# Cross-attention and scan in fp32: row tiles transposed by VectorE and SBUF-to-SBUF DMA instead of TensorE

## The chip, the core and the metric

The kernel runs on one core of one Trainium2 chip. The metric is the device time of one execution, in microseconds. Before the change it is 2022.62 us, the median of three runs (2022.18 to 2022.88).

## What is computed

All tensors are fp32. 4096 rows of 512 attend with 8 heads to 3202 context rows, then pass a recurrence with 64 states. The reference, cut to what matters:

```python
x = layernorm(rows, g1, beta1); base_n = layernorm(context, g1, beta1)
x = rows + mha(x, base_n, W_qkv, b_qkv, W_o, b_o)      # 8 heads of 64
xn = layernorm(x, g2, beta2)
U = (xn @ W_in.T + b_in) @ Bmat                         # 64 inputs a row
s = silu(s @ A.T) + u_t                                 # step after step, per batch
out = x + states @ Cmat + mod                           # mod: one row, from ctxb
```

## The kernel before

**Stages.** A first stage (to about 165 us of the span) normalises the context, makes keys and values, writes them to two DRAM tensors, kd and vd, and makes the first queries. The loop (to about 1880 us) does the attention. A tail runs the scan and writes the output.

**The loop.** The rows come in 8 blocks Q of 512 rows. A block has 4 head pairs hp of 2 halves of 256 rows: 8 units. A unit walks over 13 chunks of keys, its steps. A step is scores (L639, TensorE, sixteen 64x64 matmuls of 256 columns), weights (L709, exp on ScalarE), add (L717, the sum of the weights, on VectorE, in three of the steps on GpSimd) and, four steps later, product (L749, TensorE). At the end of a unit, fold (L724, GpSimd) adds two halves of the sum and sums (L767, TensorE, tile pd) reduces it over the keys. The adds of a unit are one chain: each reads the one before.

**Rows in and out.** For block Q+1, `queries` loads its rows in two halves of two tiles of 128 rows (x, L876), normalises them (statistics L843 on VectorE, factors L847 to L849 on GpSimd, scaling L855 on ScalarE to tile xh), has TensorE transpose them (`turn`: four 128x128 transposes a tile, L282, tile tp_x) and ScalarE copy them out of PSUM (L305); then four `heads` (L312) multiply them with the query weights. For block Q-1, `project` loads the rows again (xr, L924), adds a bias on GpSimd (L927, piece "row"), multiplies with W_o (`outs`, L933, tile pa), makes x1 (L943), stores x1 plus mod to DRAM (mod L947 on GpSimd, store L950), normalises, turns (tile tp_y) and multiplies with the scan's input weights (`inputs`, L984, tile pu). A turn of two tiles is one piece on TensorE.

**What sets the order.** The order is not written by hand. `Plan` holds pieces, each with an engine, a cost in ns, pieces that it comes after, a due time in steps (STEP = 2150 ns) and buffers that it takes and gives. `order` plays them through: a free engine takes, of the pieces that are ready, the one with the earliest due time. A due time holds nothing back: a free engine takes a ready piece early. The order of the calls that comes out is the order of the instructions on every engine; an engine then runs its own in that order and waits in front of the first that is not ready. Two details matter here. A TensorE piece of the full array (outs, turn, inputs, heads) counts as due 30,000 ns, 14 steps, later while no other of its kind could go (ALONE). And a result of SP counts as there 3000 ns after its piece (LATE). The loads of the keys and values (k, v; L1021, L1029) are no pieces: they are issued on SP where the scores of a step are placed, ten and six steps ahead. Every load, store and move here is on SP's queue.

Of the kernel before, what the change touches and what calls it, by code (L numbers as in the profile page):

```python
# [10 lines left out]
F32 = mybir.dt.float32  # L11
# [7 lines left out]

T, S2, H, NH, HD, NS = 4096, 3202, 512, 8, 64, 64  # L20
P = 128
NC = H // P
NCH = 26
CK = 128
# [3 lines left out]
QB = 512  # L28
# [141 lines left out]
def xattn_ssm_kernel(  # L170
# [114 lines left out]
        return tp[:, :, :n]  # L285

    xp_ = actx.enter_context(tc.tile_pool(name="xp", bufs=2))
    xnp = actx.enter_context(tc.tile_pool(name="xnp", bufs=2))
    qp = actx.enter_context(tc.tile_pool(name="qp", bufs=6))
    ps_m = actx.enter_context(tc.tile_pool(name="ps_m", bufs=1, space=PSUM))  # L290
    m_pools = [ps_m]
# [12 lines left out]
        yield  # L304
        nc.scalar.copy(xn[:, :, t * P : (t + 1) * P], tp)  # L305

    def heads(Q, hp, xns):

        pq = m_tile([P, 512], f"pq_{Q}_{hp}")
        for half in range(2):  # L310
            for i in range(NC):
                nc.tensor.matmul(  # L312
                    pq[:, half * QU : (half + 1) * QU],
                    wq[:, i, hp * P : (hp + 1) * P],
                    xns[half][:, i, :],
                    start=(i == 0),
                    stop=(i == NC - 1),
                )
# [7 lines left out]
    first_xns = []  # L326

    def first_queries(x0):

        xns = []  # L330
        for half in range(2):
            xn = xnp.tile([P, NC, QU], F32, tag="xn", name=f"xn_0_{half}")
            xns.append(xn)
            for t in range(NT // 2):
                name = f"x{half * QU + t * P}"
                last = normalize(x0[:, half * (NT // 2) + t, :], P, name, later=True)
                yield
                yield
                xh = last()
                yield  # L340
                yield
                for _ in turned(xn, xh, t, name):
                    yield
                yield
                yield
        first_xns.extend(xns)
        pieces = heads(0, 0, xns)
        next(pieces)
        for _ in pieces:
            yield  # L350
        yield
# [483 lines left out]
    def norm_pieces(plan, ks, gets, d, after, names, gives):  # L835
# [21 lines left out]
        for t, (k, v) in enumerate(zip(ks, vs)):  # L857
            plan.add((*k, "stats"), "DVE", 870, partial(stats_, v, gets[t], names[t]), [after[t]],
                     d + t, ["fs"])
            plan.add((*k, "factors"), "POOL", 1050, partial(factors_, v), [(*k, "stats")], d + 2000)  # L860
            plan.add((*k, "scaled"), "ACT", 800, partial(scaled_, v, gets[t], t),
                     [(*k, "factors")] + ([(*ks[0], "scaled")] if t else []), d + 3 * STEP + t,
                     [] if t else ["xh", "xh"], [("fs", (*k, "stats")), gives[t]])
        return vs

    def queries(plan, Q, d):

        xns, copied = [], []
        for half in range(2):
            ks = [("query", Q, half * 2 + t) for t in range(2)]  # L870
            at = [Q * QB + half * QU + t * P for t in range(2)]
            k2, vs, w = ("queries", Q, half), [{}, {}], {}

            def load(v, r):
                v["x"] = xp_.tile([P, H], F32, tag="x", name=f"x_{r}", bufs=4)
                nc.sync.dma_start(v["x"], x[r : r + P, :])  # L876
# [4 lines left out]
            nv = norm_pieces(plan, ks, [lambda v=v: v["x"] for v in vs], d, [(*k, "load") for k in ks],  # L881
                             [f"x{r}" for r in at], [("x", (*k, "load")) for k in ks])

            def turn(half=half, nv=nv, at=at, w=w):
                xn = xnp.tile([P, NC, QU], F32, tag="xn", name=f"xn_{Q}_{half}")
                xns.append(xn)
                w["turns"] = [turned(xn, nv[t]["xh"], t, f"x{at[t]}") for t in range(2)]
                for one in w["turns"]:
                    next(one)
# [8 lines left out]
        head_pieces(plan, Q, range(NC), xns, copied, d, QSTEP // 2,  # L898
                    [("xn", ("queries", Q, half, "turn")) for half in range(2)])

    def head_pieces(plan, Q, hps, xns, copied, d, apart, xn_):
        for hp in hps:
            v = {}

            def head(v=v, hp=hp):
                v["heads"] = heads(Q, hp, xns)
                next(v["heads"])

            plan.add(("heads", Q, hp), "PE", 3700, head, copied, d, ["m", "q"], xn_)
            plan.add(("q", Q, hp), "ACT", 590, lambda v=v: next(v["heads"], None),  # L910
                     [("heads", Q, hp)], d + STEP, [], [("m", ("heads", Q, hp))])
            d += apart

    def project(plan, Q, halves, d, index):

        for half in halves:
# [43 lines left out]
            for t in range(2):  # L960
                plan.add((*ks[t], "x1"), "DVE", 680, partial(x1_, vs[t], at[t]), [(*k2, "outs")],
                         d + STEP + t, [], [("m", (*k2, "outs"))])
            nv = norm_pieces(plan, ks, [lambda v=v: v["x1"] for v in vs], d + STEP, [(*k, "x1") for k in ks],
                             [f"y{r}" for r in at], [("x1", (*k2, "outs"))] * 2)
            for t in range(2):
                plan.add((*ks[t], "mod"), "POOL", 1280, partial(mod, vs[t]), [(*ks[t], "x1")], d + 2 * STEP,
                         [], [("x1", (*k2, "outs"))])
# [21 lines left out]
            def kept(t, w=w, at=at):  # L989
# [7 lines left out]
                    scale=2.0,  # L997
                )

            plan.add((*k2, "turn"), "PE", 1050, turn, [(*k, "scaled") for k in ks], d + 5 * STEP - now,  # L1000
                     ["m", "m", "xn2"], [("xh", (*ks[0], "scaled"))])
            for t in range(2):
                plan.add((*ks[t], "copy"), "ACT", 560, partial(copy, t),
                         [(*k2, "turn")] + ([(*ks[0], "copy")] if t else []), d + 6 * STEP + t, [],
                         [("m", (*k2, "turn"))])
            plan.add((*k2, "inputs"), "PE", 700, inputs, [(*k, "copy") for k in ks], d + 7 * STEP - now,
                     ["m"], [("xn2", (*k2, "turn"))])
            for t in range(2):
                plan.add((*ks[t], "kept"), "ACT", 280, partial(kept, t), [(*k2, "inputs")],
                         d + 8 * STEP + t, [], [("m", (*k2, "inputs"))])  # L1010
            d += 2 * RSTEP

    kts, vts = {}, {}
# [58 lines left out]
    def open_scan():  # L1072
# [2 lines left out]
        for k in (0, NS):  # L1075
            nc.sync.dma_start(t[k : k + NS], cmat)
        sv["c2"] = t
        one = xnp.tile([P, 8, NCK], F32, tag="xn", name="scan_1")
# [4 lines left out]
        two = xnp.tile([P, 1024], F32, tag="xn", name="scan_2")  # L1083
# [376 lines left out]
    def drain(plan):  # L1460
# [14 lines left out]
        plan.add("c2", "SP", 200, open_scan, [("heads", NQB - 1, NC - 1)], a0 - 6 * STEP, ["xn", "xn", "q"])  # L1475
# [208 lines left out]
    with tc.manual_schedule():  # L1684
        for g in range(AHEAD_K):
            load_k(*steps[g])
        for g in range(AHEAD):
# [1 line left out]
        plan = Plan(  # L1689
            dict(  # L1690
                s=2, m=2, mt=1, o=1, p=NP, acc=3, extra=4, q=6, x=4, x1=2, xn2=1, fs=2,
                xn=2, xh=2, max=2, rd=2, o_=12,
            ),
            dict(q=[("heads", 0, 0)], xn=[("first", half) for half in range(2)]),
        )
        head_pieces(plan, 0, range(1, NC), first_xns, [], 4 * STEP, 4 * STEP,
                    [("xn", ("first", half)) for half in range(2)])
# [109 lines left out]
```

## Time and profile before

| | |
|---|---|
| median of 3 runs | 2022.62 us |
| the profiled execution | 2022.73 us, span 2020.9 us |
| busy, share of the span | PE 98%, DVE 58%, ACT 57%, POOL 39% |
| granted TensorE clock | 0.995 of full, mean |
| DMA queue of SP and its like (q1) | 182,184 packets, 178.62 MB, 29.4% of 16 engines' span |
| loop, 165 to 1790 us | PE busy 1616.19 of 1625.00 us |
| turns in the loop | 28 (14 of tp_x, 14 of tp_y), one more at 1879.5 us |
| one block in the steady state | 218.96 us |

PE is TensorE, DVE VectorE, ACT ScalarE, POOL GpSimd, SP the engine that issues DMAs. A line of the timeline has the start in us from the span's start, the time that the line covers, the engine, the line of the kernel and the operation, and in brackets the idle time before it and what ended it. Neighbours of one kind are drawn together (x16), and such a line can hold waits inside.

### The profile page before, as it was taken

The numbers are of one execution on the slowest core, as the hardware profiler recorded it, in microseconds if no ns is written. First come the engines' busy times: TensorE is split into PE (matmuls) and PEld (weight loads), VectorE is DVE, ScalarE is ACT, GpSimd is POOL, SyncE is SP. The second block draws the span as 40 slices with busy tenths as digits, with TensorE's granted clock in tenths as the row PEclk, the third lists the DMA queues.
The fourth block names the chain that finished last, engine by engine and source line by source line (L and its number), as shares of the span: only waits on it lengthen the run. The fifth ranks groups of instructions, "written<-read, shape, count | busy, mean of one in ns | idle before, by whom it ended". The sixth has DMA issues, their size and how long they took to land.

```text
span 2020.9 us, 66912 instructions
## 1 busy us (share of the span) xinstructions
PE 1983.2 (98%) x29534; PEld 1324.9 (66%) x29534; DVE 1170.6 (58%) x1481; ACT 1160.3 (57%) x1530; POOL 789.3 (39%) x631
## 2 busy tenths in 40 slices
PE   8999999999999999999999999999999999999996
PEld 4445676776677667766677667766776667766764
DVE  4321366566665666566656666566656665666575
ACT  2233566566665566556656666556655665665653
POOL 2111244235533453245523553345324552345424
PEclk9999999999999999999999999999999999999998
DMA  5632322122222322122222222232212322444475
GB/s 169 192 99 68 99 79 83 54 80 90 88 67 78 97 79 67 55 62 93 81 59 80 90 88 67 78 96 79 67 55 62 93 81 59 144 136 129 130 208 192
DMA packets 187030, 190.66 MB, mean 94 GB/s; under 512 B 20904, under 2 KB 160168, under 8 KB 186732
## 3 DMA queue, kind: packets, MB, share of 16 engines
q1 hardware_dynamic: 182184, 178.62, 29.4%
q10 hardware_dynamic: 4548, 7.67, 1.2%
q8 instruction: 235, 3.85, 0.8%
q14 instruction: 63, 0.52, 0.1%
HBM read 156.32 MB, written 29.88 MB: 92 GB/s over the span
## 4 chain that ended last, share of the span: by engine, by line
PE 78%; DVE 10%; POOL 7%; issue 3%; ACT 1%; DMA 1%; DVEq 0%; POOLq 0%; ACTq 0%
PE po L749 27%; PE s L639 27%; DVE acc L717 6%; PE pq L312 5%; PE pk L588 4%; PE pv L555 4%; POOL acc L717 4%; PE pa L933 4%; PE pd L767 1%; DVE rd L802 1%; ACT p L709 1%; PE tp_x L282 1%; DVE acc L703 1%; POOL acc L724 1%; PE sm L657 1%
## 5 line engine op out<-in xcount | busy, mean ns | idle before, releaser
L709 ACT ACTIVATE p<-s,shifts 128x1024 f32<-128x1024 f32 (+1 forms) x832 | 894.1, 1081 | 522.8 <-PE s L639 510.4
L717 DVE TENSOR_TENSOR acc<-p,acc 128x1024 f32<-128x1024 f32 (+1 forms) x515 | 620.0, 1204 | 406.9 <-POOL acc L717 310.6
L639 PE MATMUL s<-q,k 64*64 64x256 f32 x12800 | 841.4, 378 | 2.7 <-ACT p L709 1.1
L749 PE MATMUL po<-p,v 64*64 64x256 f32 x12800 | 823.2, 376 | 0.0
L717 POOL TENSOR_TENSOR acc<-p,acc 128x1024 f32<-128x1024 f32 x189 | 446.9, 2365 | 809.1 <-DVE acc L717 484.1
L639 PEld LDWEIGHTS s<-q,k 64*64 64x64 f32 x12800 | 483.9, 133 | 217.2 <-issue 21.4
L749 PEld LDWEIGHTS po<-p,v 64*64 64x64 f32 x12800 | 489.5, 133 | 189.0 <-issue 2.2
L724 POOL TENSOR_TENSOR acc<-acc 128x512 f32<-128x512 f32 x64 | 104.5, 1633 | 135.8 <-DVE acc L717 118.0
L717 DVE TENSOR_TENSOR acc<-p,p 128x1024 f32<-128x1024 f32 x64 | 84.6, 1322 | 60.1 <-ACT p L709 54.1
L312 PE MATMUL pq<-xn,wq 128*128 128x256 f32 x512 | 119.0, 385 | 0.0
L802 DVE RECIPROCAL rd<-rd 128x256 f32<-128x256 f32 (+1 forms) x65 | 112.4, 1729 | 2.2
L312 PEld LDWEIGHTS pq<-xn,wq 128*128 128x128 f32 x512 | 94.6, 190 | 23.2 <-issue 11.6
L933 PE MATMUL pa<-wo,o 128*128 128x512 f32 x240 | 107.0, 599 | 0.0
L782 DVE TENSOR_TENSOR o<-po,o 128x256 f32<-128x256 f32 x64 | 27.2, 424 | 128.4 <-ACT o L778 128.2
L555 PE MATMUL pv<-wv,ct 128*128 128x512 f32 (+1 forms) x208 | 96.4, 616 | 1.0 <-ACT ct L523 0.7
L588 PE MATMUL pk<-ct,wk 128*128 128x512 f32 (+1 forms) x224 | 88.8, 549 | 0.0
L321 ACT ACTIVATE q<-pq,bias 128x512 f32<-128x512 f32 x32 | 22.0, 687 | 108.6 <-PE pq L312 108.6
L933 PEld LDWEIGHTS pa<-wo,o 128*128 128x128 f32 x240 | 44.4, 190 | 56.0 <-issue 55.8
L703 DVE TENSOR_TENSOR acc<-x,acc 2x256 f32<-2x256 f32 x128 | 78.1, 610 | 3.0
L523 DVE COPY ct<-tp_c 128x512 f32<-128x512 f32 (+1 forms) x13 | 8.5, 651 | 105.9 <-PE tp_c L282 105.9
L555 PEld LDWEIGHTS pv<-wv,ct 128*128 128x128 f32 (+1 forms) x208 | 38.3, 193 | 44.5 <-issue 41.7
L588 PEld LDWEIGHTS pk<-ct,wk 128*128 128x128 f32 x224 | 39.2, 190 | 42.6 <-issue 42.6
(213 smaller groups left out, 1224.1 us busy)
## 6 DMA issues: line engine op xcount, KB each, us to landing
k<-kd SPq DMA_DIRECT2D x432, 128.0 KB, 2.2
v<-vd SPq DMA_DIRECT2D x432, 128.0 KB, 2.2
xr<-in_x_dram SPq DMA_DIRECT2D x32, 256.0 KB, 4.5
x1d<-xr SPq DMA_DIRECT2D x32, 256.0 KB, 2.2
x<-in_x_dram SPq DMA_DIRECT2D x28, 256.0 KB, 3.2
cx<-in_ctx_dram SPq DMA_DIRECT2D x25, 256.0 KB, 3.0
vd<-vs SPq DMA_DIRECT2D x25, 256.0 KB, 2.4
kd<-ks SPq DMA_DIRECT2D x48, 128.0 KB, 1.8
```

The costliest lines, as they stand in the source:

```text
L312: nc.tensor.matmul(pq[:, half * QU : (half + 1) * QU], wq[:, i, hp * P : (hp + 1) * P], xns[half][:, i, :], start=(i == 0), stop=(i == NC ...
L555: nc.tensor.matmul(pv[h * HD : h * HD + n, :H], ct[:, k, o : o + n], wv[:, k, :], start=(i == 0), stop=(i == NC // parts - 1), skip_group_ ...
L588: nc.tensor.matmul(pk[:, :n_g], wk[:, i, hp * P : (hp + 1) * P], ct[:, i, :n_g], start=(i == 0), stop=(i == NC - 1),)
L639: nc.tensor.matmul(s[k0 : k0 + HD, a, b, :], kts[(*w["at"][:2], c)][r, b * CK + k0 : b * CK + k0 + HD], q[r], start=True, stop=True, skip_ ...
L703: nc.vector.tensor_tensor(to[r], t[r], to[r], ALU.add)
L709: nc.scalar.activation(t[:, :, :nb, :], w["ps"][c][:, :, :nb, :], AF.Exp, bias=w["shift"])
L717: engine.tensor_tensor(w["acc"][:, :, :nb, :], t[:, :, :nb, :], before[:, :, :nb, :], ALU.add)
L724: nc.gpsimd.tensor_tensor(acc[:, :, 0, :], acc[:, :, 0, :], acc[:, :, 1, :], ALU.add)
L749: nc.tensor.matmul(w["po"][a * HD : (a + 1) * HD, k, :QU], vts[Q, hp, c][r, b, a * HD : (a + 1) * HD], t[r, a, b, :], start=(c == 0 and b ...
L782: nc.vector.tensor_tensor(o, w["po"][:, 1, :QU], o, ALU.add)
L802: nc.vector.reciprocal(w["rd"][:, part], w["rd"][:, part])
L933: nc.tensor.matmul(v["pa"], o_t[Q, c, half][:, t * P : (t + 1) * P], wo[:, c, :], start=(c == 0), stop=(c == NC - 1),)
```

## The change

The rows of the loop (all blocks but the last one's `project`) no longer pass TensorE to be transposed. A new piece `flip` on VectorE transposes each 32x32 block of xh where it stands, into the tile that held x (or x1). Sixteen DMAs a tile then put the blocks in their places, in four pieces `move0` to `move3` on SP of four DMAs each, planned at 400 ns a piece. A DMA reads 32 partitions and writes 32 partitions, in runs of 32 numbers (128 bytes): 128 runs, 16 KB. The copies by ScalarE go too. The queries of a block are one tile of 512 columns instead of two of 256, so `heads` has half as many matmuls of twice the width. `inputs` is due 14 steps after `outs` instead of 7. The x tiles are given back after the moves instead of after the scaling, and the flip of x1 comes after mod as well.

```diff
-        for half in range(2):
-            for i in range(NC):
-                nc.tensor.matmul(
-                    pq[:, half * QU : (half + 1) * QU],
-                    wq[:, i, hp * P : (hp + 1) * P],
-                    xns[half][:, i, :],
...
+        for i in range(NC):
+            nc.tensor.matmul(
+                pq,
+                wq[:, i, hp * P : (hp + 1) * P],
+                xn[:, i, :],
...
-            plan.add((*k2, "turn"), "PE", 1050, turn, [(*k, "scaled") for k in ks], d + 4 * STEP,
-                     ["m", "m", "xn"], [("xh", (*ks[0], "scaled"))])
             for t in range(2):
-                plan.add((*ks[t], "copy"), "ACT", 560, lambda t=t, w=w: next(w["turns"][t], None),
-                         [(*k2, "turn")], d + 5 * STEP + t, [], [("m", (*k2, "turn"))])
-                copied.append((*ks[t], "copy"))
+                plan.add((*ks[t], "flip"), "DVE", 700, lambda v=vs[t], n=nv[t]: flip(v["x"], n["xh"]),
+                         [(*ks[t], "scaled")], d + 4 * STEP + t, [], [("xh", (*ks[0], "scaled"))])
+                for a in range(P // TB):
+                    first = (half, t, a) == (0, 0, 0)
+                    plan.add((*ks[t], f"move{a}"), "SP", 400, partial(move_, t, a),
+                             [(*ks[t], "flip")] + ([] if first else [("query", Q, 0, "move0")]),
+                             d + (5 + 4 * t + a) * STEP, ["xn"] if first else [], [("x", (*ks[t], "load"))])
+                    copied.append((*ks[t], f"move{a}"))
...
+    def flip(to, of):
+
+        nc.vector.transpose(to, of)
+
+    def move(xn, of, a):
+
+        for b in range(P // TB):
+            nc.sync.dma_start(
+                xn[b * TB : (b + 1) * TB, :, a * TB : (a + 1) * TB],
+                of[a * TB : (a + 1) * TB].rearrange("p (c b k) -> p b c k", b=P // TB, k=TB)[:, b],
+            )
...
-            plan.add((*k2, "inputs"), "PE", 700, inputs, [(*k, "copy") for k in ks], d + 7 * STEP - now,
-                     ["m"], [("xn2", (*k2, "turn"))])
+            if last:
...
+            else:
+                copied, xn2, after = [], (*ks[0], "move0"), 14
...
+                for t in range(2):
+                    plan.add((*ks[t], "flip"), "DVE", 700, lambda v=vs[t], n=nv[t]: flip(v["x1"], n["xh"]),
+                             [(*ks[t], "scaled"), (*ks[t], "mod")], d + 5 * STEP + t, [],
+                             [("xh", (*ks[0], "scaled"))])
+                    for a in range(P // TB):
+                        first = (t, a) == (0, 0)
+                        plan.add((*ks[t], f"move{a}"), "SP", 400, partial(move_, t, a),
+                                 [(*ks[t], "flip")] + ([] if first else [xn2]), d + (6 + 4 * t + a) * STEP,
+                                 ["xn2"] if first else [], [("x1", (*k2, "outs"))])
+                        copied.append((*ks[t], f"move{a}"))
+            plan.add((*k2, "inputs"), "PE", 700, inputs, copied, d + after * STEP - now, ["m"], [("xn2", xn2)])
```

More of the change, by code (lines that the diff above doesn't have):

```diff
@@ L21 @@
 P = 128
+TB = 32
 NC = H // P
@@ L324, in heads @@
         qt[Q, hp] = t
-    first_xns = []
+    first_xn = []
     def first_queries(x0):
[L330 to L336, printed above, removed]
-                yield
[L338 to L347, printed above, removed]
+        xn = xnp.tile([P, NC, QB], F32, tag="xn", name="xn_0")
+        first_xn.append(xn)
+        for t in range(NT):
+            name = f"x{t * P}"
+            last = normalize(x0[:, t, :], P, name, later=True)
+            yield
+            yield
+            xh = last()
+            yield
+            yield
+            for _ in turned(xn, xh, t, name):
+                yield
+            yield
+            yield
+        pieces = heads(0, 0, xn)
         next(pieces)
@@ L881, in queries @@
             nv = norm_pieces(plan, ks, [lambda v=v: v["x"] for v in vs], d, [(*k, "load") for k in ks],
[L882 to L889, printed above, removed]
@@ L901, in head_pieces, with move_ @@
-    def head_pieces(plan, Q, hps, xns, copied, d, apart, xn_):
+                             [f"x{r}" for r in at], [])
+            def move_(t, a, half=half, vs=vs):
+                if (half, t, a) == (0, 0, 0):
+                    w["xn"] = xnp.tile([P, NC, QB], F32, tag="xn", name=f"xn_{Q}")
+                c0 = (half * 2 + t) * P
+                move(w["xn"][:, :, c0 : c0 + P], vs[t]["x"], a)
+            for t in range(2):
+                plan.add((*ks[t], "flip"), "DVE", 700, lambda v=vs[t], n=nv[t]: flip(v["x"], n["xh"]),
[6 more added lines that the diff above has]
+                    copied.append((*ks[t], f"move{a}"))
@@ L1077, in open_scan @@
         sv["c2"] = t
-        one = xnp.tile([P, 8, NCK], F32, tag="xn", name="scan_1")
+        both = xnp.tile([P, 2, 1024], F32, tag="xn", name="scan")
+        one = both[:, 0, :].rearrange("p (i k) -> p i k", k=NCK)
         sv["th"] = [one[:, i, :] for i in range(2)]
@@ L1082, in open_scan @@
         sv["ok"] = one[:, 7, :]
-        two = xnp.tile([P, 1024], F32, tag="xn", name="scan_2")
+        two = both[:, 1, :]
         at_ = 0
```

58 lines of the change are left out of this document (32 added, 26 removed).

## The prediction

> **What bounds it now.** First the busy times on the page, then the list of what TensorE waited for:
>
> ```profile
> PE 1983.2 (98%) x29534; PEld 1324.9 (66%) x29534; DVE 1170.6 (58%) x1481; ACT 1160.3 (57%) x1530; POOL 789.3 (39%) x631
> ```
>
> ```profile
> PE pd L767 <- POOL acc L724: 4.9, 6, 0.8
> ```
>
> TensorE is the bound: 1616.19 of 1625.00 us in the loop. So work taken from it counts in full. But the second line (4.9 us in total, 6 times, 0.8 at the longest) is a warning: six times, once a block, `sums` already waits for the fold on GpSimd. There the chain of adds has no slack, and whatever delays it is paid by TensorE. I then read the timeline around the first block's turn, engine by engine. TensorE:
>
> ```profile
> 477.79 1.04 PE L639 MATMUL s<-q,k 64*64 64x256 f32 x16
> 478.77 1.09 PE L282 MATMUL tp_y<-ident,xh_y 128*128 128x128 f32 x8
> 479.79 1.57 PE L639 MATMUL s<-q,k 64*64 64x256 f32 x24
> 481.19 1.04 PE L749 MATMUL po<-p,v 64*64 64x256 f32 x16
> 482.05 1.04 PE L639 MATMUL s<-q,k 64*64 64x256 f32 x16
> ...
> 489.19 0.76 PE L767 MATMUL pd<-acc,ones 64*64 64x256 f32 x8 [0.81 <-POOL acc L724]
> ```
>
> Differences of the starts are what things cost: sixteen quarter matmuls 0.86 us (481.19 to 482.05).
>
> **What TensorE gains.** A turn takes 1.02 us (478.77 to 479.79). The scores ahead of it take 0.98 instead of 0.86, the 24 behind it 1.40 instead of 1.29: entering and leaving the full array is 0.23. Each of the 28 turns of the loop stands alone like this, so 28 x 1.25 = 35.0 us. A head: sixteen matmuls of 256 columns take 3.65 us (577.71 to 581.36), 0.228 each; sixteen of 512 columns (tile pa, 464.52 to 471.58) take 7.06, 0.441 each. Eight of those are 3.53, so 32 heads give 32 x 0.12 = 3.8 us. Together **38.8 us**. The profiled execution took 2022.73 us (span 2020.9 and 1.8 around it), 0.1 above the median; with nothing else it would come to 1984.
>
> **What is added off TensorE.** VectorE gets 56 flips. No such operation is in the trace. The nearest rows are VectorE's fp32 operations on 128x512: 0.48 (scaling a weight) to 0.75 us; the dearest kind, the reciprocal, takes 1.73 for 256 columns, so 3.5 is the other end. I take 0.7, as in the nearest rows: 39 us in all on an engine idle for 42% of the span; ScalarE loses 56 copies of 0.59. The idle time that hides a flip of x1 is 5.43 us from 476.26 to 481.69. At 3.5 us that cover would be gone, and the chain below would start 3 us later.
>
> **What SP gets** is the point: 56 x 16 = 896 DMAs. SP's timeline after `outs` (which ends at 471.6):
>
> ```profile
> 472.65 2.90 SPq L950 DMA_DIRECT2D x1d<-xr  x2
> 475.64 0.38 SPq L1021 DMA_DIRECT2D k<-kd  x1
> 476.12 0.40 SPq L1029 DMA_DIRECT2D v<-vd  x1
> 476.61 0.38 SPq L1021 DMA_DIRECT2D k<-kd  x1
> 477.08 0.38 SPq L1029 DMA_DIRECT2D v<-vd  x1
> 477.57 0.84 SPq L876 DMA_DIRECT2D x<-in_x_dram  x2
> ...
> 481.30 1.10 SPq L924 DMA_DIRECT2D xr<-in_x_dram  x2
> ```
>
> Back to back, one DMA follows another by 0.48 us, whether it carries 2 KB or 256 KB. No move of 32 partitions is in the trace; nearest are two DMAs into 64 partitions (tile a_t, 0.48 and 0.58 on ScalarE's queue) and one of 2 partitions (vx, 0.73). I take 0.48: 16 moves are 7.7 us, where the planner counts 1.6. As data they are light: the trace's packets last 28 ns at 512 B and 9 ns at 16 B, so eight runs of 128 B on each of 16 engines are 0.07 to 0.22 us, under the pitch. That two DMAs into parts of one tile need not wait for one another, a_t shows: issued 0.7 us apart, landing after 5.2.
>
> One rule of the Trainium skill speaks against this weight: DMA: Bandwidth & Descriptors, Issuing engines are not separate DMA queues, calls the sequencer's time to start a DMA usually small beside the DMA itself. For one k load the trace agrees (0.48 to issue, 2.2 to land); for 16 in a row the issue is 7.7. By that rule the moves would hold nothing up, and the time would be the 1984 of the first rival.
>
> **Where the moves stand in SP's order.** Due times don't spread them: a free engine takes a ready piece early. The scaling of the first tile ends at 474.79, VectorE is free at 476.26, so its flip ends near 477.0. The x loads of the next queries are released by the scores just before tp_y (477.79 to 478.77), the xr loads two to three steps later. The second tile's scaling ends at 478.20, its flip near 478.9. So the planner lays out: stores, first 16 moves, x loads, second 16 moves, xr loads, with the k and v of the steps between. Now the real times: stores until 475.55, a pair of k and v to 476.5, flip 477.0, 16 moves 7.7, two pairs 1.9, so the x loads go at 486.6 instead of 477.57, **9 us late**. Then x loads 1.0, 16 moves 7.7, two pairs 1.9: the xr loads go at 497.2 instead of 481.30, **16 us late**.
>
> **Who waits for them.** The loads' landings, and then VectorE and GpSimd, each in order:
>
> ```profile
> xr<-in_x_dram SPq DMA_DIRECT2D x32, 256.0 KB, 4.5
> ...
> x<-in_x_dram SPq DMA_DIRECT2D x28, 256.0 KB, 3.2
> ```
>
> ```profile
> 482.83 0.69 DVE L843 BATCH_NORM_STATS2 st_x<-x 128x6 f32<-128x512 f32 x1
> ...
> 484.45 0.66 DVE L717 TENSOR_TENSOR acc<-p,acc 128x512 f32<-128x512 f32 x1
> ```
>
> ```profile
> 487.87 1.26 POOL L724 TENSOR_TENSOR acc<-acc 128x512 f32<-128x512 f32 x1
> 489.09 2.51 POOL L927 TENSOR_TENSOR xr<-xr,rowb 128x512 f32<-128x512 f32 x2
> 491.55 2.38 POOL L717 TENSOR_TENSOR acc<-p,acc 128x1024 f32<-128x1024 f32 x1
> ```
>
> The statistics of x stand on VectorE in front of the last half add of a unit (484.45); that add releases the fold (487.87), the fold `sums` (489.19). The x loads landed at 481.6 (478.41 + 3.2), 1.2 us before they were needed. Nine late less 1.2: `sums` is **7.8 us** late, all of it TensorE's. Behind the fold, GpSimd adds the bias to xr (489.09), and only then comes the next unit's first add of its own (491.55), from which that unit's chain runs without a gap to its fold (ends 511.77; `sums` at 512.99, slack 1.2). The xr loads land at 497.7 + 4.5 = 502.2, so the row adds start 13.1 late; TensorE is 7.8 late already and the slack is 1.2: **4.1 more**. That is 11.9 a block, for the six blocks with both loads: 71. The last block has no queries: xr alone, one us earlier, 12.1 - 1.2 = 10.9. Together 82 us.
>
> **The rest at nothing.** The k and v of the loop are issued 13 steps, some 25 us, ahead of their use (the buffer's last reader is three steps before the issue, the use ten after); with SP late by 16 that still covers; past 25 us every further one would be lost. `inputs` stood 13.1 us after `outs` with 7 steps; with 14 it stands near 496, or 493 if another full-array piece is ready, and the second 16 moves land near 499.4 (497.2 + 2.2): 3 to 6 us short, but TensorE is 7.8 late by then and does not notice. In the blocks' second halves the x loads stand right behind the stores, ahead of the moves, and `inputs` is the only one near its limit (moves land near 551, place near 550): 0 to 5 us seven times, taken as 0. `heads` has 11 steps to spare.
>
> **Sum:** 2022.7 - 38.8 + 82 = **2066 us**.
>
> **Rivals.**
> 1. *Faster: SP's burst is hidden* (0.20), 1984 to 2010. For it: SP is idle or waiting for half of a block, VectorE and GpSimd have idle time, and TensorE's waits are tiny. It decides whether 16 moves hold the loads by less than the 1.2 us of slack: a pitch under 0.1 us, or x and xr loads ahead of the moves. Against it: the pitch of 0.48 in every row, and the 0.81 wait at `sums`. If only the x loads come ahead, xr alone still costs 13.1 - 1.2 a block, and the result stays with the forecast.
> 2. *TensorE waits at* `inputs` *for the moves instead* (0.07): loads in time, but 5 us at each of 14: 1984 + 70 = 2054.
> 3. *The moves are dearer* (0.12): 128-byte runs of 0.1 us each, or waits between the moves, make a pitch of 0.8. Then x is 14 late and xr 26, some 23 us a block: 1984 + 7 x 23 = 2145, more where k and v run out.
> 4. Gain and stalls cancel to within 0.2% (0.03).
>
> The forecast itself has 0.58 (its own range 2035 to 2100: one tile's burst shorter or longer by 2 us moves a block by 4). Faster is rival 1, 0.20; same 0.03; slower the rest, 0.77; 0.2% is about what a measurement here can tell from no change. The range takes in half of rival 1 and of rival 3: 1988 to 2140.
>
> **What would show it.** TensorE's busy time falls to some 1948 us (30.8 of transposes, 4 of heads), its waits for the fold (pd) grow from 4.9 to about 80 us. SP shows runs of 16 moves of 7.7 us; VectorE's st_x waits for the DMA of x, GpSimd's L927 for xr. Wrong would be: runs of moves much shorter or longer, x and xr loads at their old distance from `outs`, or the wait at pu.

## The result, and the profile after

The changed kernel takes **2335.84 us** (median of 4 runs, 2333.85 to 2336.48) against 2022.4 of the kernel before beside it: 1.155 times as long, 95% interval 1.1528 to 1.1568. The forecast was 2066 with a range of 1988 to 2140. The sign was right, the size was not: 313 us where the forecast had 43.

First the busy times on the page, which answer to the line of before (PE 1983.2, 98%), and the list of what TensorE waited for:

```profile
PE 2043.5 (88%) x29054; PEld 1285.7 (55%) x29054; DVE 1208.8 (52%) x1537; ACT 1133.4 (49%) x1474; POOL 786.1 (34%) x631
```

```profile
PE pu L995 <- DMA xn<-x: 148.2, 21, 12.8
PE po L746 <- DMA v<-vd: 58.7, 15, 5.9
PE s L636 <- DMA k<-kd: 33.1, 6, 6.2
```

Two things stand here. TensorE has 480 instructions less and yet is busy 60.3 us longer; and its waits are for three kinds of DMA, of which only one, the moves (xn<-x), is new. The wait for the fold (pd, 4.9 us before), which the forecast expected to grow to 80, is no longer in the list.

The accounts close: the span grew by 312.8 us. TensorE's idle time in it went from 37.7 to 290.2 (+252.5; the three lines above are 240.0 of that), its busy time by +60.3.

SP's timeline after `outs`, which ends at 476.4 in this profile (471.6 before):

```profile
481.77 5.59 SPq L906 DMA_DIRECT2D xn<-x  x8
...
488.52 5.11 SPq L906 DMA_DIRECT2D xn<-x  x8
493.68 1.07 SPq L873 DMA_DIRECT2D x<-in_x_dram  x2
494.85 2.52 SPq L906 DMA_DIRECT2D xn<-x  x4
...
498.91 7.67 SPq L906 DMA_DIRECT2D xn<-x  x12
...
508.68 0.90 SPq L934 DMA_DIRECT2D xr<-in_x_dram  x2
...
512.05 23.11 SPq L906 DMA_DIRECT2D xn<-x  x32
535.27 0.53 SPq L1059 DMA_DIRECT2D v<-vd  x1
```

The order is the forecast's: 16 moves, x loads, 16 moves, xr loads. The pitch is not: 0.63 us a move in the short runs (2.52 by 4), 0.70 in the first (5.59 by 8), 0.72 in the last (23.11 by 32), against 0.48 taken. And in the last line but one 32 moves of the queries stand without a break, with a load of v behind them. TensorE over the same stretch:

```profile
495.49 0.40 PE L995 MATMUL pu<-xn,wc 128*64 128x128 f32 x2 [2.99 <-DMA xn<-x]
507.86 1.97 PE L995 MATMUL pu<-xn,wc 128*64 128x128 f32 x14 [11.97 <-DMA xn<-x]
509.76 1.81 PE L764 MATMUL pd<-acc,ones 64*64 64x256 f32 x5
...
537.23 1.13 PE L746 MATMUL po<-p,v 64*64 64x256 f32 x8 [5.00 <-DMA v<-vd]
```

In brackets is the idle time ahead of a row. TensorE stands before `inputs` (pu) for 2.99 and 11.97 us, until the two tiles' moves have landed, and only then comes to `sums` (pd), which has nothing left to wait for. Before, `inputs` stood ahead of `sums` as well (484.75 and 489.19), and its sixteen matmuls followed the work ahead of them without a wait:

```profile
484.75 1.09 PE L984 MATMUL pu<-xn,wc 128*64 128x128 f32 x16
```

The v that was issued at 535.27, behind the 32 moves, costs another 5.00.

Last the windows of this stretch. The columns: the stretch and its length, the busy time of PE, PEld, DVE, ACT and POOL with their instructions in brackets, then the clock that TensorE was granted, the share of the DMAs and their GB/s:

```profile
508.00:512.00 4.00, 3.99 (x28) 2.48 (x32) 0.00 (x0) 2.06 (x3) 0.00 (x0) 0.50 0.95 272
512.00:520.00 8.00, 8.00 (x145) 5.13 (x144) 5.04 (x6) 5.22 (x8) 4.83 (x3) 0.93 0.34 86
520.00:532.00 12.00, 12.00 (x230) 7.99 (x222) 6.48 (x7) 7.39 (x7) 4.75 (x2) 1.00 0.16 27
537.00:541.00 4.00, 3.77 (x44) 2.30 (x48) 0.42 (x1) 1.23 (x2) 0.94 (x1) 0.58 0.44 130
```

Behind the gap of 12 us TensorE works at 0.50 of its clock for 4 us, then recovers; behind the gap of 5.00 it is 0.58. The same work shows it: 14 matmuls of `inputs` take 1.97 us behind the gap, 16 of them took 1.09 before. That is where the longer busy time comes from, and nothing in the prediction had it.

### The profile page after: what moved, and what is told of

Its sections match the earlier page's. It is cut to its first block, busy times and chain, and to the rows that moved or that the text cites. A ratio compares the mean times of both kernels' runs of the same rounds, so it can differ in the third digit from the quotient of the medians.

```text
span 2333.7 us, 67163 instructions
## 1 busy us (share of the span) xinstructions
PE 2043.5 (88%) x29054; PEld 1285.7 (55%) x29054; DVE 1208.8 (52%) x1537; ACT 1133.4 (49%) x1474; POOL 786.1 (34%) x631
## 3 DMA queue, kind: packets, MB, share of 16 engines
q10 hardware_dynamic: 4548, 7.67, 1.1%
## 4 chain that ended last, share of the span: by engine, by line
PE 53%; SPq 20%; DVE 10%; POOL 7%; issue 5%; DMA 2%; ACT 2%; DVEq 0%; POOLq 0%; ACTq 0%
PE s L636 18%; SPq L906 17%; PE po L746 17%; DVE acc L714 6%; PE pq L312 4%; POOL acc L714 4%; PE pk L585 4%; PE pv L552 4%; PE pa L943 2%; ACT p L706 1%; SPq L1059 1%; DMA v<-vd 1%; DVE rd L799 1%; SPq L1051 1%; POOL xr L957 1%
## 5 line engine op out<-in xcount | busy, mean ns | idle before, releaser
L636 PE MATMUL s<-q,k 64*64 64x256 f32 x12800 | 891.6, 388 | 47.6 <-DMA k<-kd 33.1
L746 PE MATMUL po<-p,v 64*64 64x256 f32 x12800 | 878.5, 388 | 58.7 <-DMA v<-vd 58.7
L636 PEld LDWEIGHTS s<-q,k 64*64 64x64 f32 x12800 | 511.6, 137 | 297.9 <-issue 85.0
L746 PEld LDWEIGHTS po<-p,v 64*64 64x64 f32 x12800 | 516.0, 138 | 273.4 <-DMA v<-vd 64.3
L995 PE MATMUL pu<-xn,wc 128*64 128x128 f32 x240 | 35.3, 406 | 148.2 <-DMA xn<-x 148.2
L312 PE MATMUL pq<-xn,wq 128*128 128x512 f32 x256 | 118.3, 605 | 0.0
L714 DVE TENSOR_TENSOR acc<-p,p 128x1024 f32<-128x1024 f32 x64 | 90.9, 1420 | 52.0 <-ACT p L706 46.4
L995 PEld LDWEIGHTS pu<-xn,wc 128*64 128x64 f32 x240 | 25.8, 209 | 158.0 <-issue 108.1
L585 PE MATMUL pk<-ct,wk 128*128 128x512 f32 (+1 forms) x224 | 88.8, 549 | 0.0
L312 PEld LDWEIGHTS pq<-xn,wq 128*128 128x128 f32 x256 | 46.0, 189 | 57.5 <-issue 57.5
L937 POOL TENSOR_TENSOR xr<-xr,rowb 128x512 f32<-128x512 f32 x30 | 44.5, 1510 | 95.1 <-DMA xr<-in_x_dram 95.1
```

The source lines that it names most:

```text
L312: nc.tensor.matmul(pq, wq[:, i, hp * P : (hp + 1) * P], xn[:, i, :], start=(i == 0), stop=(i == NC - 1),)
L585: nc.tensor.matmul(pk[:, :n_g], wk[:, i, hp * P : (hp + 1) * P], ct[:, i, :n_g], start=(i == 0), stop=(i == NC - 1),)
L636: nc.tensor.matmul(s[k0 : k0 + HD, a, b, :], kts[(*w["at"][:2], c)][r, b * CK + k0 : b * CK + k0 + HD], q[r], start=True, stop=True, skip_ ...
L714: engine.tensor_tensor(w["acc"][:, :, :nb, :], t[:, :, :nb, :], before[:, :, :nb, :], ALU.add)
L746: nc.tensor.matmul(w["po"][a * HD : (a + 1) * HD, k, :QU], vts[Q, hp, c][r, b, a * HD : (a + 1) * HD], t[r, a, b, :], start=(c == 0 and b ...
```

## The experiments

Theory A, in its first form: the 313 us come from the number of DMAs issued one after another on SP, and from what they hold up, with TensorE's clock on top. The rivals: the transfers themselves (short runs), the flips on VectorE, the wider heads, the place of `inputs` in the plan. All times are medians; before was 2022.4 to 2022.9 beside each. "Gaps" are TensorE's pauses of 3.4 us or more between 300 and 2000 us of the trace; "at 0.50" counts the stretches of the same part of the trace in which its granted clock was 0.50 (the two of e2 lie in its tail). e3, e4, e5, e6, e8, e12 and e15 were run once, the others four times or more.

| kernel | moves' DMAs | us | TensorE busy | clock | gaps | at 0.50 |
|---|---|---|---|---|---|---|
| before | 0 | 2022.4 | 1983.2 | 0.995 | 0 | 0 |
| after | 896 | 2335.84 | 2043.5 | 0.934 | 31 | 31 |
| e1_wide_heads | 0 | 2021.87 | 1980.8 | 0.996 | 0 | 0 |
| e2_no_moves | 0 | 2007.04 | 1954.7 | 0.995 | 0 | 2 |
| e3_rows_only | 448 | 2269.39 | 2007.0 | 0.947 | 20 | 12 |
| e4_queries_only | 448 | 2085.08 | 1990.7 | 0.982 | 10 | 12 |
| e5_act_queue | 896, ScalarE's queue | 2341.51 | 2023.8 | 0.942 | 14 | 17 |
| e6_cost | 896 | 2223.89 | 1996.6 | 0.951 | 19 | 19 |
| e7_blocks | 0 | 2162.44 | 2015.7 | 0.961 | 8 | 32 |
| e8_long_runs | 896 | 2312.47 | 2047.7 | 0.940 | 24 | 31 |
| e9_bounce | 280 | 2047.22 | 1969.4 | 0.989 | 0 | 5 |
| e10_split | 0 | 2189.61 | 2001.9 | 0.957 | 25 | 14 |
| e11_cost_late | 896 | 2204.33 | 2005.1 | 0.957 | 15 | 22 |
| e12_late | 896 | 2321.45 | 2020.4 | 0.933 | 25 | 22 |
| e13_loads_early | 896 | 2227.71 | 1994.8 | 0.947 | 14 | 13 |
| e14_warm | 896 | 2343.54 | 2149.9 | 0.960 | 23 | 24 |
| e15_early_only | 896 | 2352.39 | 1995.8 | 0.925 | 25 | 14 |

### The parts of the change: e1, e2, e3, e4

**e1_wide_heads** puts the turns and copies of before back and keeps the one buffer for the queries of a block, with matmuls of 512 columns in the heads.

```diff
-plan.add((*ks[t], "flip"), "DVE", 700, ...)   # and the 16 moves
+plan.add((*k2, "turn"), "PE", 1050, turn, ...)
+plan.add((*ks[t], "copy"), "ACT", 560, partial(copy, t), ...)
```

> The change without flips and moves: rows still transposed by TensorE, but the queries of a block in one buffer and the heads as half as many matmuls of 512 columns. Theory (the loss comes from the moves on SP): the heads are worth what the rows of before give, 32 x 0.12 us, so 2018.6 us, 3.8 below before. Rival (the one buffer costs, because all four heads wait for both halves): above 2022.

Measured 2021.87, ratio 0.9996 (0.9986 to 1.0005). The wide heads are worth nothing that can be measured: one takes 3.63 us (576.27 to 579.90) against 3.65 before.

**e2_no_moves** lets the flip write straight into the tile's place, without DMAs.

```diff
-nc.sync.dma_start(xn[...], of[...])            # 16 a tile
+flip(w["xn"][:, :, c0 : c0 + P], nv[t]["xh"].rearrange("p (c k) -> p c k", c=NC))
```

> The change without the 896 moves: the flip writes straight into the tile that the matmuls read, so the 32x32 blocks are transposed but stay in the wrong places and the output is another. Everything else is as in the change. Theory (SP's moves cause the loss): TensorE keeps its gain of 38.8, 1984 us, mean clock back near 0.99, no wait at pu. Rival (the flips on VectorE hold the chain of adds): well above 2022, with waits at pd.

Measured 2007.04, ratio 0.9924 (0.9908 to 0.9941). So the moves cost 2335.84 - 2007.04 = **329 us**, and flips, freed TensorE and heads together give 15 us, where 38.8 were forecast. TensorE's busy time fell by 28.5; its idle time rose by 12.3, and a new wait heads its list:

```profile
PE s L636 <- ACT p L706: 15.0, 26, 0.8
```

Here `s` waits for ScalarE's exponentials to free a buffer: with the turns gone, the step is ScalarE's and VectorE's in places. That is the next bound.

**e3_rows_only** and **e4_queries_only** use flips and moves on one side, turns on the other.

> Flips and moves for the rows after attention only; the queries are turned by TensorE and copied by ScalarE (one wide buffer). Theory (bursts of 32 moves on SP, each about 0.7 us): the waits at pu stay (148 us in the change, plus the slow clock behind them), the waits for k and v (92 us) go, since no second burst follows: 2130 to 2220 us. Rival (the DMA engines are crowded by 128-byte packets): half the packets, so about half of the loss over 1984 everywhere, near 2160 with waits at k and v too.

> Flips and moves for the queries only; the rows after attention are turned by TensorE. Theory (bursts on SP): no wait at pu, heads have steps to spare, and one burst of 32 alone is covered by the lead of the k and v loads: 2000 to 2040 us. Rival (crowded DMA engines): near 2160, waits for k and v as in the change.

Measured 2269.39 and 2085.08, a single run each: +247 and +62, together 309 of the 313. Both lay above what was expected of them; that 32 query moves would be covered by the lead of the k and v loads was wrong. Same number of DMAs, a fourfold difference: the price is not a price per move but what waits for it. In e3 TensorE stands 203.5 us ahead of `inputs` and never for k or v; in e4 it stands 56.6 us for v and never for the moves, which `heads` needs later.

### Transfers or their number: e8, e9

**e8_long_runs** issues the same 896 moves of 16 KB with runs of 512 bytes instead of 128.

```diff
-xn[b * TB : (b + 1) * TB, :, a * TB : (a + 1) * TB],
+xn[b * TB : (b + 1) * TB, a, :],
```

> The change with the same 896 moves of 16 KB between 32 partitions, but each reads and writes one run of 512 bytes a partition instead of four of 128 (a quarter of the packets, one dimension less); the blocks land in other places, so the output is another. Theory A (what counts is the number of DMAs): SP's distance from move to move stays near 0.70 us and the time near 2336. Theory B (short runs make a move dearer to issue): the distance falls to the 0.48 of other DMAs, and 2336 falls to 2150 or lower. Theory C (128-byte packets crowd the DMA engines): the time falls though the distance stays.

Measured 2312.47: 23 us less, of 329. In its trace 32 moves in a row take 22.43 us, against 23.11. So the pitch of 0.70 us hardly depends on the runs. The data are light as well: the 114,688 packets of 128 bytes in the changed kernel's trace last 12 ns each, so a move of 128 runs, shared evenly by the 16 DMA engines, would be about 0.1 us on each.

**e9_bounce** moves the blocks through DRAM: five DMAs a tile.

```diff
+for a in range(P // TB):
+    nc.sync.dma_start(v["d"][:, :, a].rearrange("b i e -> i b e"),
+                      of[a * TB : (a + 1) * TB].rearrange("i (b e) -> i b e", b=P // TB))
+...
+nc.sync.dma_start(xn.rearrange("p a c k -> p (a c k)"), v["d"].rearrange("b i a e -> (b i) (a e)"))
```

> The blocks go to their place through DRAM: per tile four writes of 32 partitions and one read of 128 (5 DMAs instead of 16, twice the bytes), the blocks of a tile kept in an order in which runs are 512 bytes, and the read planned after the writes have landed. The heads and `inputs` then read their queries and rows in runs of 32. Theory A (number of DMAs on SP): 280 instead of 896, some 6 us for a pair of tiles instead of 21; 2010 to 2060. Theory B (the way through memory and its bytes, not the number): two landings instead of one and twice the bytes, above 2150.

Measured 2047.22, ratio 1.0114 (1.0097 to 1.0131), within the range of theory A: 40 us above the kernel without DMAs, with twice the bytes and two landings. Its plan differs too (a piece of four writes counts 2000, and the read is planned after they land), so number and plan are not separated by this run alone. No gap of 3.4 us is left. It is the fastest way with the blocks put in place, and it takes 1.1% longer than the kernel before.

### Other ways around SP: e5, e7, e10

**e5_act_queue** issues the moves from ScalarE, planned at 2600 a piece of four.

```diff
-nc.sync.dma_start(
+nc.scalar.dma_start(
```

> The change with the 896 moves issued by ScalarE instead of SP (planned there at 2600 ns a piece of four). Theory (SP's queue is what is held up): x, xr, k and v loads go on time, the waits for k and v (92 us) go; the issue time, about 0.65 us each, now sits on ScalarE, 580 us on top of 1133, so ScalarE holds scores: 2050 to 2200 us. Rival (the DMA engines or their rings are crowded): the waits for k and v stay, 2250 or more.

Measured 2341.51, outside the 2050 to 2200 expected, though TensorE's waits for k and v are gone, as the theory had it. Its ScalarE timeline says why:

```profile
487.34 18.47 ACTq L906 DMA_DIRECT2D xn<-x  x28
505.91 1.11 ACT L706 ACTIVATE p<-s,shifts 128x1024 f32<-128x1024 f32 x1 [17.82 <-DMA xn<-x]
```

28 moves take 18.47 us there too, 0.66 each, and the exponential behind them comes 17.82 us late. TensorE waits ahead of `inputs` (168.2) and of `s` (88.7). The pitch is not SP's own, and ScalarE has more to lose.

**e7_blocks** lets VectorE transpose each block straight to its place, 16 instructions a tile; **e10_split** plans them as four pieces of 1230 instead of one of 3500.

```diff
+for a in range(P // TB):
+    for b in range(P // TB):
+        nc.vector.transpose(to[b*TB:(b+1)*TB, :, a*TB:(a+1)*TB], of[a*TB:(a+1)*TB, :, b*TB:(b+1)*TB])
```

> The change without DMAs and with the right output: VectorE transposes each 32x32 block straight into its place, 16 instructions of 32 partitions x 128 a tile instead of one, planned at 3500 ns a tile. No nearer row than the flip (0.71 us for 512 columns): at 0.2 us each they are 3.2 us a tile, 180 us on VectorE. Theory (the moves are the loss, and what is left of the gain hangs on the chain of adds): between the run without moves (2007) and some 20 to 40 us above it, 2010 to 2050. Rival (VectorE becomes the bound): above 2100.

> VectorE transposes each block of 32x32 straight to its place, as in the run with sixteen transposes a tile, but planned at what they took (1.21 us a group of four, four pieces a tile, where one piece of 3.5 us stood for 4.8). Theory C (VectorE's order is what hurt: a piece of 4.8 us stood ahead of the sums of p and the normalising of o): 2040 to 2090. Theory D (VectorE's 135+135 us do not fit between the sums): within 1 per cent of that run's 2162.

Measured 2162.44 (ratio 1.0688, 1.067 to 1.0706) and 2189.61 (1.0817, 1.0795 to 1.0839). In e7's groups:

```profile
L901 DVE STREAM_TRANSPOSE xn<-xh_x 32x128 f32<-32x128 f32 x448 | 135.5, 302 | 9.0 <-ACT xh_x L852 3.1
L901 DVE STREAM_TRANSPOSE xn<-xh_y 32x128 f32<-32x128 f32 x448 | 135.5, 302 | 7.4 <-ACT xh_y L852 1.2
```

A quarter of the partitions and of the columns costs 302 ns, against 711 for the whole tile: 16 x 0.302 = 4.83 us a tile. The time is on the side of e7's rival (above 2100), though VectorE is busy only 68%: TensorE waits 46.5 us for the adding of po to o and 35.8 us for the fold. The finer plan made it worse, so neither theory of e10 holds as put (C wanted 2040 to 2090, D within 1 per cent of 2162); how VectorE's queue would have to be ordered stays open.

### The plan: e6, e12, e11, e15, e13

**e6_cost** plans a piece of four moves at 2700 instead of 400, its real time.

> The change with one number altered: a piece of four moves is planned at 2700 ns instead of 400. Theory (the planner puts inputs where it believes 32 moves to be done after 3.2 us, and the chip needs 23): inputs are placed later, the 148 us of waits at pu shrink to under 50, with the slow clock behind them; the k and v loads are still held: 2100 to 2200 us. Rival (SP's capacity, whatever the order): unchanged within 20 us of 2336.

Measured 2223.89, a little above. The plan now puts k and v between the fours, and the wait for v is gone from the list, that for k down to 9.0 us ahead of `s`. The cost moves `inputs` in TensorE's order: in the first half of a block TensorE reaches it 30.5 us after `outs`, where it was 16.0. That is still too early. With the loads of k and v between them the first 32 moves take 30.8 us (473.17 to 503.92) where the plan counts 21.6. So the wait ahead of `inputs` is still 137.8, not under 50 as expected, and `heads` now waits for moves as well (35.0).

**e12_late** leaves the cost at 400 and makes `inputs` due ten steps later; **e11_cost_late** does both, sixteen steps.

```diff
-copied, xn2, after = [], (*ks[0], "move0"), 14
+copied, xn2, after = [], (*ks[0], "move0"), 24      # e12; 30 and cost 2700 in e11
```

> All 896 moves as in the changed kernel; only the due time of the product `inputs` after the rows' moves is ten steps later. In the changed kernel TensorE stood 195.8 us ahead of `inputs` until a move landed, 27 times. Theory A (the moves are issued one at a time on SP, 32 in 21 to 23 us; `inputs` stands in TensorE's order where the plan believes them landed after about 6 us): the wait ahead of `inputs` goes, most of the 95 us of slower clock behind the gaps with it, the waits for k and v (92 us) stay: 2060 to 2140. Theory B (SP's own time is the bound, whatever the order): the wait comes back ahead of k, v or the sums, and the time stays above 2250.

> Both corrections to the plan: a piece of four moves costs 2700 instead of 400, and `inputs` is due sixteen steps later. With the cost alone (2224) TensorE still stood 197.0 us ahead of `inputs`, and no longer for v. Theory A: the remaining wait is only where `inputs` stands; 2224 less 197 and some 20 of clock, so 2000 to 2040, which is the kernel without the moves (2007) within 30. Theory B (SP's own time): above 2120, with the wait at k, v or the queries' heads.

The 195.8 and 197.0 in these texts are from the view of the one line, which counts more of the idle time than the list of waits (148.2 and 137.8). e12: 2321.45, and 193.6 us still ahead of `inputs`. Theory A's forecast for it fell, but not for theory B's reason: in TensorE's order `inputs` stayed where it was, 16.0 us after `outs` in the first halves, behind the same run of 32 scores; only `sums`, which came right after it, moved further back. A due time ranks the pieces that are ready; the plan believes the moves landed, and takes `inputs` as soon as they are.

e11: 2204.33, ratio 1.0901 (1.0883 to 1.0919). The wait ahead of `inputs` is gone wholly, and another stands in its place, which is theory B's side, though ahead of `s` and not, as that theory had it, of k, v or the heads. TensorE's list, then VectorE's:

```profile
PE s L636 <- ACT p L706: 127.8, 32, 10.1
```

```profile
DVE st_x L840 <- DMA x<-in_x_dram: 139.0, 18, 11.5
```

and the chain from one to the other, engine by engine:

```profile
507.99 0.69 DVE L840 BATCH_NORM_STATS2 st_x<-x 128x6 f32<-128x512 f32 x1 [9.86 <-DMA x<-in_x_dram]
```

```profile
511.13 0.81 ACT L852 ACTIVATE xh_x<-x,nm_x,rstd_x 128x512 f32<-128x512 f32 x1 [10.52 <-POOL nm_x L846]
```

```profile
513.00 1.99 PE L636 MATMUL s<-q,k 64*64 64x256 f32 x16 [9.46 <-ACT p L706]
```

The x loads are issued at 505.03, behind the rows' moves. VectorE stands 9.86 us at the statistics, ScalarE 10.52 at the scaling that needs them, the exponentials behind the scaling are late, and `s` has no free buffer. This is the chain of the prediction, one queue further on: it had the wait pass through VectorE and GpSimd to `sums`, and here it goes through ScalarE to `s`.

**e15_early_only** makes the loads of x for queries and rows due and held to 14 steps ahead instead of 2 and 4; **e13_loads_early** does so on top of e11.

```diff
-[from_(d - 2 * STEP)], d - 2 * STEP, ["x"])     # rows: d - 4 * STEP
+[from_(d - 14 * STEP)], d - 14 * STEP, ["x"])
```

> The changed kernel with only the loads of x made 14 steps ahead instead of 2 and 4. If the late loads of x were a cause of their own from the start (VectorE 58 us at the statistics, GpSimd 95 us at the rows): 2290 to 2310. If they hide behind the wait ahead of `inputs`, as the changed kernel's waits of TensorE say: 2325 to 2340.

> As the run with the cost of 2700 and a later `inputs` (2204), and the loads of x for queries and rows due and held to 14 steps ahead instead of 2 and 4. In that run the wait had moved: x loads issued behind the moves, VectorE 139 us at the statistics for them, ScalarE behind it at the scaling, TensorE 127.8 us at s for p. Theory A (the moves' cost is only what they put behind them on SP; with the three orders mended little is left): 2030 to 2080. Theory B (SP has no room for 896 moves in the order it can be given; each order mended shows the next wait): the wait moves once more, to k, v or the heads, and the time stays above 2120.

e15: 2352.39, somewhat above the band for loads that hide behind `inputs`; TensorE stands 305.5 us ahead of `inputs` in its groups, and for v not at all. e13: 2227.71, above e11, theory B's number. The longest wait stays where e11 had it, ahead of `s` (100.2 in 15 waits, up to 16.1 each), and part of the one ahead of `inputs` is back (81.7); VectorE still waits 119.7 us for x, whose loads stand at 521.30, again behind the moves. The earlier due did not bring them ahead; why is not shown (the four buffers of x, which query tiles now hold until their moves are issued, were not tried).

So five plans give 2204 to 2352: e6, e12 and e15 with their longest wait ahead of `inputs`, e11 and e13 ahead of `s`. That no order could do better is not shown.

### The clock: e14

**e14_warm** fills TensorE's gap ahead of `inputs` with 40 matmuls whose result is written over.

```diff
+for _ in range(40 if Q < NQB - 1 else 0):
+    nc.tensor.matmul(w["pu"], ident, ident, start=True, stop=True, skip_group_check=True)
```

> The changed kernel with 40 matmuls of 128x128 by 128x128, whose result is written over, put ahead of `inputs` where TensorE stands idle for 14 us on average, in the first seven blocks; about 40 x 0.27 = 10.9 us of work in each of 14 gaps. If TensorE's slower clock behind the gaps comes from the gaps themselves, the gaps for the rows are now 3 us, and some two thirds of the 95 us that the same work took longer come back: 2275 to 2300, with a mean clock of 0.955 or more. If the slower clock comes from something else (the DMAs, the load on the other engines): the clock of the windows behind `inputs` stays at 0.5, and the time at 2336 or above.

Measured 2343.54; the time expected was wrong, and both theories' marks were met in part: the clock rose to 0.960, the time did not fall. Two windows tell it. In the first block the filling was too short and 6.54 us of gap were left; in its second half it was long enough:

```profile
500.00:506.00 6.00, 0.00 (x0) 0.00 (x0) 1.33 (x3) 1.07 (x2) 1.48 (x2) 0.71 0.16 25
506.00:508.00 2.00, 1.96 (x15) 1.63 (x16) 0.00 (x0) 0.00 (x0) 0.00 (x0) 0.50 0.83 238
...
508.00:512.00 4.00, 4.00 (x31) 2.01 (x34) 0.85 (x2) 3.83 (x8) 1.98 (x2) 0.50 0.91 284
```

```profile
583.00:585.00 2.00, 2.00 (x32) 1.55 (x34) 0.00 (x0) 0.54 (x2) 0.00 (x0) 1.00 0.22 42
```

Within the 6 us of gap the clock drops (0.71 on average), and the next 6 us of work run at 0.50. Without a gap, in the second fence, it stays at 1.00 with moves running beside it, where the changed kernel had 0.50 at the same place (582 to 584, behind 5.92 us). So the gap is the cause here, and 6 us of it are nearly as bad as 12. The time did not fall because the filling itself ran 128.8 us and took only 104.2 us of the wait away.

How much a gap costs is another matter. By busy time above e2's 1954.7, the changed kernel needs 88.8 us more for 31 gaps, and e14, without its filling, 66.4 for 23: 2.9 a gap in both. The table shows that this agreement is luck. The same count gives 1.6 a gap in e15 (41.1 for 25) and 7.6 in e7 (61.0 for 8). The granted clock itself says what is paid. In all these traces it is either 1.00 or 0.50, and the stretches at 0.50 last 3.41 us or a multiple of it. TensorE worked 4.90 us in such a stretch on average in the changed kernel, 4.97 in e14, 5.00 in e15 and 3.66 in e7. Half of that is lost: 1.8 to 2.5 us a stretch. So the loss goes by the number of these stretches, neither by the number nor by the length of the gaps, and a stretch needs no long gap. In e7, with no DMA at work:

```profile
574.59 5.40 PE L312 MATMUL pq<-xn,wq 128*128 128x512 f32 x8 [1.56 <-DVE xn L901]
```

```profile
571.50:574.90 3.40, 1.47 (x21) 0.81 (x18) 3.25 (x11) 2.50 (x3) 0.00 (x0) 1.00 0.00 0
575.00:578.30 3.30, 3.30 (x5) 1.35 (x4) 3.27 (x4) 0.00 (x0) 1.27 (x1) 0.50 0.00 0
```

TensorE was busy for 1.47 of 3.40 us, its longest pause was 1.56, and the head behind it, at 0.50 from 575.00 to 578.30, covers 5.40 us instead of e1's 3.70. e9 has five such stretches with no pause above 3.39 us.

## Why the prediction was wrong, step by step

**TensorE's gain, 38.8: mis-sized.** The heads' 3.8 are not there (e1: 0.8, inside the interval). I had divided the time of sixteen matmuls of 256 columns and halved that of sixteen of 512; the head measured 3.63 against 3.65. The turns gave 1980.8 - 1954.7 = 26 us of busy time, not 35.0, and e2 less e1 is 15 us of time. The missing 11 are waits for ScalarE and VectorE (15.0 us for the exponentials where e1 has 1.1): "counts in full" holds only while TensorE is the bound in every stretch.

**The flips: right.** 697 to 712 ns, taken 0.7; bounds 0.48 and 3.5.

**The moves, 0.48 each: mis-sized.** 0.63 to 0.72. The row taken was one of 128 partitions from or to DRAM. Two DMAs into 64 partitions of SBUF stood beside it at 0.48 and 0.58, and two partitions at 0.73; their mean, 0.60, would have been nearer. (Nor is 0.48 the same "whether it carries 2 KB or 256 KB": behind the two 2 KB loads on SP the next DMA comes after 0.37.) The last move for the first `inputs` was issued by 506.6, 30 us after `outs`, against 25.6 forecast. Light as data they were, about 0.1 us each (e8).

The rule that was weighed against this step, in the Trainium skill (DMA: Bandwidth & Descriptors, Issuing engines are not separate DMA queues: the time on the sequencer is usually small), does not hold here for runs of DMAs. One move takes 0.63 us to issue and 1.8 to land; but 896 moves, up to 32 in a row, cost 329 us, and longer runs of bytes took back only 23.

**SP's order: right** in its sequence, with k and v falling inside the runs of moves; the x loads 11 us late (forecast 9), the xr loads 22.5 late (forecast 16).

**Who waits: the step that failed.** "`inputs` ... stands near 496", behind `sums`, "TensorE is 7.8 late by then and does not notice". It stands ahead of `sums`, as it had before, and TensorE reached it at 492.5, 16 us after `outs`, not 24. I had used the rule that a free engine takes a ready piece early for SP, and not for TensorE: the plan counts 3.2 us for the 32 moves of two tiles, which took SP 20.9 (5.59, 5.11, 2.52 and 7.67), so it believes them landed some 18 us too soon. TensorE stood 15.0 us there in the first block, 106 in the seven first halves, and what the late loads of x and xr did to `sums` was hidden behind it. The second halves, "0 to 5 us seven times, taken as 0", came to 4.9 to 8.5 each, 42 in all. The place comes from readiness and not from the due time: ten steps more leave it at 16.0 us after `outs` (e12), the real cost of the moves puts it at 30.5 (e6). e11 shows that the forecast's chain through x is real, once `inputs` is out of its way.

**k and v at nothing: failed.** "[P]ast 25 us every further one would be lost": 32 query moves alone hold SP for 23.11 us, on top of the delay that was there, so 91.8 us were lost. The prediction had looked at the rows' moves and given the queries' "11 steps to spare"; that held for `heads`, which waited for nothing, and not for the loads queued behind.

**Not in the prediction: the clock**, some 82 to 89 us, as much as the whole stall that it forecast. The larger number is busy time above e2's; by the clock records TensorE lost 86.8 us at 0.50 in the changed kernel and 5.0 in e2, a difference of 82. The Trainium skill, TensorE: Matmul & The Clock Gate, Part 1: The HAM clock gate, has it: half rate after an idle window of about 3.4 us, full rate again after as long. The traces agree on the half rate (0.50 behind 11.97, 0.58 on average behind 5.00) and on the length (3.41 us or a multiple). They differ on what brings it: in e7 a stretch of 3.4 us in which TensorE was busy for 1.47 was enough. In the loop of the kernel before no pause passed 1.1 us, so the loop could not show it. Its tail does: behind a pause of 2.38 us, ending at 1999.92, TensorE was granted half of its clock.

```profile
2000.10:2006.80 6.70, 4.94 (x50) 3.12 (x47) 5.42 (x19) 1.39 (x5) 1.47 (x2) 0.50 0.46 161
```

Of the rivals, 2 (the wait at `inputs`) and 3 (a pitch of 0.8, "more where k and v run out") both came, together: 15 us at a first `inputs`, 10.6 on average over the 14, and a pitch of 0.7. Each had been priced alone, against a full clock: 2054 and 2145. The wait at pu was also among the prediction's own signs of being wrong.

The sum as it turned out, on the span: 148.2 ahead of `inputs`, 91.8 for k and v, 12.5 of other idle time, 88.8 of slower work (82 of it at half clock by the records), less 28.5 of removed work: 312.8.

## What to carry to other kernels

When a planned piece becomes many instructions on a queue, put its real issue time into the plan first and ask on every engine, not on the queue alone, which piece the plan will now take too early; then look at everything that is queued behind. A burst of small DMAs costs by what stands behind it, so count DMAs and bursts, not bytes. And where a bound engine will be made to wait, ask how often as well as how long: here each stretch at half clock behind such waits cost some 2.4 us more.

## What the runs showed of the hardware

- A DMA between partitions of SBUF with 32 partitions of 512 bytes is issued every 0.63 to 0.72 us, on SP and on ScalarE's queue (0.66), with runs of 128 or 512 bytes alike; the writes of 32 partitions to DRAM in e9 follow one another by 0.45 to 0.77 (e9's SP rows of four in the first block: 1.78 to 3.09).
- A transpose in blocks on VectorE takes 0.71 us for 128x512 in fp32, and 0.302 for 32x128.
- TensorE's granted clock is 1.00 or 0.50 in these traces. The stretches at 0.50 last 3.41 us or a multiple, behind pauses of 12 us as behind 5 to 6, and in e7 behind one of 1.56 in a stretch of 3.40 us with 1.47 of work. They cost 1.8 to 2.5 us each in the four kernels worked out above.
- In e9 TensorE is busy 14.7 us longer than in e2 with no gap of 3.4 us; its clock records have 16.0 us lost at 0.50, against e2's 5.0, so 11 of the 14.7.
